# Short score packs of two sequences in one bank, and an earlier send of the second sequence's probabilities, in a latent-attention kernel

## The chip, the cores and the metric

The kernel runs on one core of a Trainium2 chip, in float32. The metric is the device time of one execution in microseconds (us). Five engines work side by side, each through its own list of instructions in order: TensorE (PE in the profile; PEld is its weight load), VectorE (DVE), ScalarE (ACT), GpSimd (POOL) and SyncE (SP, which here only issues transfers). They wait for each other by semaphores. Matrix products go into PSUM banks, from which DVE and ACT read.

## The reference

The input x is 16 sequences of 256 tokens with 256 features. Two layers run one after the other, and each adds (mixer of the normalised x) × silu(feed-forward net of the normalised x) to x. The first layer's mixer is a linear recurrence, and its net a GELU network. The second layer, in which the change lies, has this mixer:

```python
q = (x @ Wq).reshape(B, S, N_HEADS, QK_DIM)             # 16 heads, 128 + 64
q = concatenate([q_nope, apply_rope(q_rope)])
c_kv, k_rope = split(x @ Wkv_a)                         # latent 64, rope 64
k_nope, v = split((rms_norm(c_kv) @ Wkv_b).reshape(...))
scores = einsum('bqhd,bkhd->bhqk', q, k) * scale        # causal mask, softmax
out = einsum('bhqk,bkhd->bqhd', attn, v).reshape(B, S, N_HEADS * V_DIM)
return out @ Wo
```

and, as its net, a linear map with low-rank expert corrections chosen by a router.

## The kernel before

**Tiling.** The 4096 tokens are cut into 8 chunks (`NCH`) of 512 tokens, two sequences each. The kernel multiplies the key and value projections into the query and output weights, so that keys and values are the 64 latent numbers, and a key has 128 rows (64 latent, 64 rope). The 16 heads go in 4 groups of 4. One **unit** is one group of one sequence: 64 units, i = 8 × chunk + r, where even r is the first sequence of the chunk and odd r the second. The main loop has one turn per unit, here called a **slot**, r0 to r7. Later slots of a chunk also carry the router, the keys and the normalisation of the next chunk, and the output product of the chunk before (`fast_begin`, `fast_end`).

**Scores of a unit.** The queries of four heads × 32 positions stand on 128 partitions; there are 8 such query blocks. Block a sees 32·(a + 1) keys, as the mask is causal. The blocks go in three packs, each into one PSUM tile named sc (pool of 3 banks):

```python
PACK = (((7, 0), (6, 256)), ((5, 0), (4, 192), (3, 384)), ((2, 0), (1, 96), (0, 192)))
```

Pack 2, the short one, has blocks of 96, 64 and 32 keys. `score_pack` issues the products of a pack on PE, then on DVE one mask addition and a maximum per block (nm<-sc), then on ACT an exp per block, which writes the probabilities (pr) and their sum (sr). In even slots after i = 4 the short pack is issued as two 64-column tiles per product (128*64 in the profile), elsewhere at full width (128*128). `normalise` inverts sr on DVE and multiplies pr by it on POOL, block by block. pr has two buffers, one for each parity of the unit.

**From probabilities to values.** In the slot after its scores, a unit's pr is turned by three DVE stream transposes (`turn`, with z = 1, 2 from packs 0 and 1, and z = 0 from the short pack), into `turned`. `send` writes it to DRAM in four transfers (far<-turned), and `fetch` brings it back in another layout (pT<-far), two transfers per sequence and group. `values_of` then multiplies both sequences' pT with the values (av), in the even slot that lies two after the group's own. The last two units do the same with PE transposes (`turn_here`).

**Queries.** The products of a group's queries (pq) are made one to three slots ahead, four of them in an even and the odd slot before it: two are multiplied with the rotation on DVE (`query_mul`), added on POOL (`query_rot`, qrot), and brought to their partitions by eight transfers (`query_move`, qg<-qrot); the other two are scaled into qg by ACT (`query_lat`).

**Order.** The helper `InOrder` keeps each engine's instructions in the order in which the program names them, so the loop body is the schedule. All recorded operations carry the helper's line, L53, so groups are told apart by tile names. SP issues sends, fetches and moves from one queue; there are eight semaphores for them in rotation, so a transfer is issued only after the one eight before it has landed. m1, the pool of all other products, has 5 banks.

In the order of one slot: query_move of the group two slots on (even) and fetches; pack 0; normalise of the unit before (pack 2); parts of the gate, the next chunk's layer norm (`norm_end`, in r2 of chunks 1 to 6) and keys; turns 1 and 2 of the unit before; a query product; pack 1; turn 0 and send; in even slots values_of and another fetch; pack 2; normalise (packs 0 and 1); the rest.

Of the kernel before, what the change touches and what calls it, by code (L numbers as in the profile page):

```python
# [11 lines left out]
F32 = mybir.dt.float32  # L12
# [6 lines left out]
P = 128  # L19
B, S, D = 16, 256, 256  # L20
NTOK = B * S
CH = 512
# [19 lines left out]
def tile_two_layers(ctx: ExitStack, tc: tile.TileContext, d: dict, out: bass.AP):  # L42
# [54 lines left out]
    pe = InOrder(nc.tensor)  # L97
# [132 lines left out]
    chunks = [Chunk() for _ in range(NCH)]  # L230
# [150 lines left out]
    NQ = S // 32  # L381
# [4 lines left out]
    groups = [Group() for _ in range(NCH * NG)]  # L386
# [43 lines left out]
    def query_move(n):  # L430
        q = groups[n]
        for r in range(2):
            for h in range(G):
                sp.dma_start(
                    q.qg[64 + 32 * r : 96 + 32 * r, :, h, :],
                    q.rot[32 * h : 32 * h + 32, r, :].rearrange("p (a q) -> p a q", q=32),
                )


    with ExitStack() as l0:  # L440
# [151 lines left out]
        u = tiny("u")  # L592
        f = tiny("f")
# [24 lines left out]
        for k in range(8):  # L618
            n = 1 << k
# [612 lines left out]
        o = out1  # L1232
# [126 lines left out]
    class Unit:  # L1359


        def __init__(self, i):
            self.i = i
            self.ch, r = divmod(i, 2 * NG)
            self.g, self.b = divmod(r, 2)
            self.n = f"{self.ch}_{self.g}_{self.b}"
            self.pr = prs[i % NPR]

    def score_pack(u, pi):
        k, b, pack = chunks[u.ch], u.b, PACK[pi]  # L1370
        if pi == 0:
            u.nm = sm1.tile([P, NQ], F32, tag="nm", name=f"nm_{u.n}", bufs=3)
            u.sr = sm1.tile([P, NQ], F32, tag="sr", name=f"sr_{u.n}", bufs=3)
        qg = groups[u.i // 2].qg
        sc = ps_sc.tile([P, CH], F32, tag="sc", name=f"sc_{u.n}_{pi}")
        halves = 2 if pi == 2 and u.b == 0 and u.i > 4 else 1
        m = P // halves
        for a, o in pack:
            w = qg[:, b * NQ + a, :, :].rearrange("p h q -> p (h q)")
            for y in range(halves):  # L1380
                pe.matmul(
                    sc[m * y : m * y + m, o : o + 32 * (a + 1)], w[:, m * y : m * y + m],
                    k.kT[:, b * S : b * S + 32 * (a + 1)], start=True, stop=True,
                )
        ends = [o + 32 * (a + 1) for a, o in pack]
        step = ends[1] - ends[0]
        n = len(pack)
        assert ends == [ends[0] + step * z for z in range(n)]
        if ends[0] - 32 + step * n <= CH:
            diag = sc[:, ends[0] - 32 : ends[0] - 32 + step * n].rearrange("p (n s) -> p n s", n=n)[:, :, 0:32]  # L1390
        else:
            diag = sc[:, ends[0] - step : ends[-1]].rearrange("p (n s) -> p n s", n=n)[:, :, step - 32 : step]
        ve.tensor_tensor(diag, diag, bc(kmask, n), ALU.add)
        for a, o in pack:
            ve.tensor_reduce(
                u.nm[:, a : a + 1], sc[:, o : o + 32 * (a + 1)], AX.X, ALU.max, negate=True
            )
        for a, o in pack:
            w = 32 * (a + 1)
            ac.activation(  # L1400
                u.pr[:, OFF[a] : OFF[a] + w], sc[:, o : o + w], AF.Exp,
                bias=u.nm[:, a : a + 1], accum_out=u.sr[:, a : a + 1],
            )

    def normalise(u, packs):
        blocks = [a for pi in packs for a, _ in PACK[pi]]
        lo, hi = min(blocks), max(blocks) + 1
        ve.reciprocal(u.sr[:, lo:hi], u.sr[:, lo:hi])
        for a in blocks:
            v = u.pr[:, OFF[a] : OFF[a] + 32 * (a + 1)]  # L1410
            gp.tensor_scalar(v, v, u.sr[:, a : a + 1], 1.0, ALU.mult, ALU.mult)
# [6 lines left out]
    def turn(u, z):  # L1418
        if z == 1:
            u.turned = pp.tile([P, 4, 3, P], F32, tag="turned", name=f"turned_{u.n}", bufs=2)  # L1420
        a0, k0 = THIRDS[z]
        o, w = OFF[a0], WID[a0]
        ve.transpose(
            u.turned[:, :, z, :].rearrange("p k (a q) -> p a k q", q=32),
            u.pr[:, o : o + 4 * w].rearrange("p (a k s) -> p a k s", a=4, s=32)[
                :, :, k0 : k0 + 4, :
            ],
        )
# [15 lines left out]
    def fetch(n, y, b):  # L1444

        q = groups[n]
        if y == b == 0:
            q.pT = {}
        if b == 0:
            q.pT[y] = pp.tile([P, G, 3 * P], F32, tag="pT", name=f"pT_{n}_{y}", bufs=3)  # L1450
        sp.dma_start(
            q.pT[y][64 * b : 64 * b + 64].rearrange("p h q -> p (h q)"),
            q.far[b].rearrange("(y k) s h z q -> y (k s) (h z q)", y=2)[y],
        )

    def turn_here(u, z):

        if z == 1:
            new_pT(u)
        a0, k0 = THIRDS[z]  # L1460
        pt = m1(f"pt_{u.n}_{z}", [P, CH])
        for y in range(4):
            o = OFF[a0] + y * WID[a0] + 32 * k0
            pe.transpose(pt[:, y * P : (y + 1) * P], u.pr[:, o : o + P], ident)
        for y, e in ((0, ac.copy), (2, ve.tensor_copy)):
            e(
                u.pT[:, :, z, 32 * y : 32 * y + 64].rearrange("p h (a q) -> p a h q", q=32),
                pt[:, y * P : (y + 2) * P].rearrange("p (a h q) -> p a h q", a=2, h=G),
            )
# [183 lines left out]
    for i in range(LAST):  # L1653
        ch, r = divmod(i, PER)
        odd = i % 2 == 1
        u, w = units[i], units[i - 1] if i else None
        here = w is not None and w.i >= LAST - 2
        n = (i + 3) // 2 if odd else (i + 2) // 2
        n = n if n < len(groups) else None
        more = ch + 1 < NCH  # L1660
        last = ch - 1 if ch == NCH - 1 and r in FINISH else None
        fast = ch - 1 if 0 < ch < NCH - 1 else None

        if not odd and n is not None:
            query_move(n)
        if odd and i > 2:
            fetch((i - 3) // 2, 0, 1)
            fetch((i - 3) // 2, 1, 1)
        elif i and not odd:
            fetch((i - 2) // 2, 0, 0)  # L1670
        score_pack(u, 0)
        if w:
            normalise(w, (2,))
        if fast is not None and r > 3:
            fast_begin(fast, r)
        if ch > 1 and r == 0:
            fast_begin(ch - 2, 0)
        out_weights(i)
        if r == 1:
            gate_end(ch, 0)  # L1680
        if r == 2:
            gate_end(ch, 1)
            if more and ch:
                norm_end(ch + 1)
        if r == 5 and more:
            kv_end(ch + 1)
        if i == LAST - 1:

            finish_mm(last, 3, 0, NPAIR)
            finish_out(last, 3)  # L1690
            last = None
        if w:
            for z in (1, 2):
                turn_here(w, z) if here else turn(w, z)

        if r == 0:
            mid_chunk(ch)
        if r == 7 and more:
            key_chunk(ch + 1)
        if n is not None:  # L1700
            query_mm(n, 0 if odd else 3)
            if not odd:
                query_lat(n, 3)
        if i == 5:
            values_of(0)
        score_pack(u, 1)

        if odd and n is not None:
            query_mm(n, 1)
            query_mul(n, 0)  # L1710
        if w:
            if here:
                turn_here(w, 0)
            else:
                turn(w, 0)
                send(w)
        if not odd:
            if i > 4:
                values_of((i - 4) // 2)
            if i:  # L1720
                fetch((i - 2) // 2, 1, 0)
        score_pack(u, 2)
        normalise(u, (0, 1))

        if odd and n is not None:
            query_mm(n, 2)
            query_mul(n, 1)
            query_rot(n)
            query_lat(n, 2)
        if r < 2:  # L1730
            gate_begin(ch, r)
        if r == 0 and more and ch:
            norm_begin(ch + 1)
        if r == 2 and more:
            transpose_chunk(ch + 1)
        if r == 4 and more:
            kv_begin(ch + 1)
        if r == 6 and more:
            router_chunk(ch + 1)
        if last is not None:  # L1740
            j = FINISH.index(r)
            finish_mm(last, j, 0, NPAIR)
            finish_out(last, j)
        if fast is not None and r in FINISH:
            fast_end(fast, r)
# [1 line left out]

    ch = NCH - 1
    u0, u1 = units[LAST - 2], units[LAST - 1]
    normalise(u1, (2,))  # L1750

    finish_mm(ch, 0, 0, 4)
    finish_mm(ch, 1, 0, 4)
# [86 lines left out]
```

## Time and profile before

| | |
|---|---|
| median of 3 runs | 903.97 us (903.92 to 904.76) |
| profiled execution | 903.67 us, its span 901.9 us |
| mean granted TensorE clock | 0.994 |
| attention part, first to last slot | 266.49 us to the end |
| one chunk, r0 to r7 (412.71 to 491.50) | 78.79 us |
| slots r0 to r7 of that chunk | 9.41, 10.04, 7.65, 11.03, 11.73, 11.03, 8.23, 9.67 us |

A slot is counted here from PE's first product of its pack 0 to that of the next. The other rows are single instructions or groups on the profile's clock, which starts with the span. A row such as "427.19 0.75 PE … x6" gives the start, the time until the last modelled end, and the number of records; since products overlap in the array, the time that a group holds PE is read from its start to the start of what follows.

### The profile page before, as it was taken

How to read it: one execution, taken by the hardware profiler on the slowest of the kernel's cores; microseconds unless marked ns; L12 is line 12 of the kernel's file. 1: busy time of each engine (PE TensorE's matmuls, PEld its weight loads, DVE VectorE, ACT ScalarE, POOL GpSimd, SP SyncE). 2: the span in 40 equal slices, each digit the busy share in tenths (PEclk: the TensorE clock that was granted, in tenths of full speed). 3: DMA queues.
4: the chain of work that ended last, by engine and by line, in shares of the span. 5: the costliest groups of instructions: out<-in, count | busy, mean ns of one | idle time of the engine just before them, and what ended most of it. 6: DMA issues, size and time to landing. Idle time of an engine off the chain costs nothing.

```text
span 901.9 us, 17976 instructions
## 1 busy us (share of the span) xinstructions
PE 889.3 (99%) x5688; PEld 666.8 (74%) x5688; DVE 667.4 (74%) x2017; ACT 476.0 (53%) x1562; POOL 571.2 (63%) x885
## 2 busy tenths in 40 slices
PE   9999999999999989999999999999999999999988
PEld 8777999987757657776776777677677767766766
DVE  6886678764687869678868867886886788687642
ACT  3234665644436646655655565565556556556441
POOL 2229687787355537787586677758667775876531
PEclk9999999999999999999999999999999999999989
DMA  9730000000024888887887887788788768878880
GB/s 276 245 118 1 1 2 1 1 1 1 1 32 79 230 209 198 186 207 161 217 218 169 206 181 201 180 217 214 170 200 211 190 170 209 210 176 194 209 223 29
DMA packets 197406, 134.04 MB, mean 149 GB/s; under 512 B 143104, under 2 KB 187968, under 8 KB 197312
## 3 DMA queue, kind: packets, MB, share of 16 engines
q1 hardware_dynamic: 195184, 128.69, 58.0%
q0 software_dynamic: 1152, 3.67, 1.2%
q8 instruction: 46, 0.75, 0.4%
q10 hardware_dynamic: 976, 0.53, 0.2%
q14 instruction: 48, 0.39, 0.1%
HBM read 63.11 MB, written 52.95 MB: 129 GB/s over the span
## 4 chain that ended last, share of the span: by engine, by line
PE 93%; DVE 3%; DMA 2%; POOL 1%; ACT 1%; SPq 0%; issue 0%; ACTq 0%; POOLq 0%
PE pq L53 23%; PE sc L53 14%; PE po L53 11%; PE av L53 8%; PE f L53 7%; PE r L53 7%; PE pg L53 5%; PE ph L53 5%; PE pf L53 5%; PE pm L53 2%; PE pkv L53 2%; PE tp L53 2%; DMA far<-turned 1%; DMA pT<-far 1%; PE pb L53 1%; PE py L53 1%
## 5 line engine op out<-in xcount | busy, mean ns | idle before, releaser
L53 POOL TENSOR_SCALAR pr<-pr,sr 128x256 f32<-128x256 f32 (+7 forms) x512 | 192.5, 397 | 188.2 <-DVE sr L53 180.3
L53 ACT ACTIVATE pr<-sc,nm 128x256 f32<-128x256 f32 (+7 forms) x512 | 190.2, 382 | 217.1 <-DVE sr L53 139.6
L53 PEld LDWEIGHTS sc<-kT,qg 128*128 128x128 f32 (+1 forms) x1198 | 150.8, 176 | 54.8 <-issue 41.6
L53 PE MATMUL sc<-kT,qg 128*128 128x32 f32 (+6 forms) x1198 | 169.0, 290 | 0.0
L53 DVE TENSOR_REDUCE nm<-sc 128x1 f32<-128x256 f32 (+7 forms) x512 | 127.5, 301 | 6.6
L53 DVE STREAM_TRANSPOSE turned<-pr 128x512 f32<-128x512 f32 x186 | 123.2, 687 | 11.0 <-POOL pr L53 10.9
L53 PE MATMUL pq<-xnT,wlat 128*128 128x512 f32 x256 | 122.7, 602 | 0.0
L53 PE MATMUL pq<-xnT,wrope 128*128 128x512 f32 x256 | 120.2, 593 | 0.0
L53 ACT ACTIVATION_READ_ACCUMULATOR pr<-sc,nm 128x1 f32 x512 | 104.0, 203 | 0.0
L53 PE MATMUL av<-pT,rowv 64*64 64x512 f32 (+2 forms) x992 | 80.5, 445 | 6.0 <-DMA pT<-far 6.0
L53 POOL TENSOR_TENSOR qrot<-qmul,qmul 128x512 f32<-128x512 f32 x64 | 83.6, 1329 | 2.8 <-DVE qmul L53 2.8
L53 DVE TENSOR_TENSOR sc<-sc,kmask 128x96 f32<-128x96 f32 (+1 forms) x192 | 45.2, 236 | 53.8 <-PE sc L53 52.5
L53 DVE TENSOR_TENSOR qmul<-pq,rot_q 128x512 f32<-128x512 f32 x128 | 80.7, 672 | 0.1
L53 ACT ACTIVATE qg<-pq 64x512 f32<-64x512 f32 x128 | 75.5, 590 | 4.3 <-PE pq L53 3.5
L53 PEld LDWEIGHTS av<-pT,rowv 64*64 64x64 f32 x992 | 39.8, 135 | 43.6 <-issue 30.1
L53 PEld LDWEIGHTS pq<-xnT,wrope 128*128 128x128 f32 x256 | 45.7, 191 | 32.4 <-issue 32.1
L53 PEld LDWEIGHTS pq<-xnT,wlat 128*128 128x128 f32 x256 | 45.7, 191 | 31.6 <-issue 31.6
L53 PEld LDWEIGHTS po<-wout,attT 128*128 128x128 f32 x416 | 59.3, 193 | 9.8 <-issue 3.5
L53 PE MATMUL po<-wout,attT 128*128 128x128 f32 (+1 forms) x416 | 65.3, 311 | 0.0
L53 POOL TENSOR_TENSOR attT<-attT,attT 128x512 f32<-128x512 f32 x36 | 45.1, 1273 | 0.0
L53 POOL TENSOR_TENSOR rs<-ve,mhalf 128x4 f32<-128x4 f32 (+1 forms) x17 | 16.8, 987 | 41.1 <-DVE ve L53 33.6
L53 PE MATMUL pf<-p2T,hT 128*128 128x256 f32 x192 | 42.7, 380 | 0.0
(229 smaller groups left out, 1520.0 us busy)
## 6 DMA issues: line engine op xcount, KB each, us to landing
far<-turned SPq DMA_DIRECT2D x248, 192.0 KB, 4.4
pT<-far SPq DMA_DIRECT2D x124, 384.0 KB, 4.9
qg<-qrot SPq DMA_DIRECT2D x256, 64.0 KB, 2.7
x<-in_x_dram SPq DMA_DIRECT2D x7, 512.0 KB, 10.4
out_dram<-x POOLq DMA_DIRECT2D x12, 256.0 KB, 4.0
wqn_wo<-in_wq_nopeT_dram SPq DMA_DIRECT2D x4, 512.0 KB, 5.4
wqn_wo<-in_Wo_dram SPq DMA_DIRECT2D x4, 512.0 KB, 6.8
p2T<-in_proj2T_dram SPq DMA_DIRECT2D x2, 512.0 KB, 8.3
```

The costliest lines, as they stand in the source:

```text
L53: r = getattr(self.engine, name)(*args, **kw)
```

## The change

`score_pack` is cut into `score_mm` (products) and `score_exp` (mask, maxima, exps). Every short pack is now issued in two 64-column tiles. A new function, `score_small(u, v)`, runs in each even slot: it takes one bank for the short pack of the even unit u (from column 0) and of the next odd unit v (from column 256), issues the 12 + 12 tiled products, and then mask, maxima and exps of u, and after them those of v. Odd slots have no short pack.

The order changes with it. An even slot does all three turns of the odd unit before it ahead of pack 1, and sends it; only then come query_move and the fetch that stood at the slot's start. An odd slot normalises the short packs of both units at its start, since both were made in the even slot before. The tail's normalise of the last unit's short pack falls away.

```diff
+    def score_mm(u, pi, sc, base=0):
+        k, b = chunks[u.ch], u.b
+        qg = groups[u.i // 2].qg
+        m = P // 2 if pi == 2 else P
+        for a, o in PACK[pi]:
+            w = qg[:, b * NQ + a, :, :].rearrange("p h q -> p (h q)")
+            for y in range(0, P, m):
+                pe.matmul(
+                    sc[y : y + m, base + o : base + o + 32 * (a + 1)], w[:, y : y + m],
+                    k.kT[:, b * S : b * S + 32 * (a + 1)], start=True, stop=True,
+                )
...
+    def score_pack(u, pi):
+        sc = ps_sc.tile([P, CH], F32, tag="sc", name=f"sc_{u.n}_{pi}")
+        score_mm(u, pi, sc)
+        score_exp(u, pi, sc)
+
+    def score_small(u, v):
+
+        sc = ps_sc.tile([P, CH], F32, tag="sc", name=f"sc_{u.n}_2")
+        for z, y in enumerate((u, v)):
+            score_mm(y, 2, sc, z * S)
+        for z, y in enumerate((u, v)):
+            score_exp(y, 2, sc, z * S)
...
-        if not odd and n is not None:
-            query_move(n)
         if odd and i > 2:
             fetch((i - 3) // 2, 0, 1)
             fetch((i - 3) // 2, 1, 1)
-        elif i and not odd:
-            fetch((i - 2) // 2, 0, 0)
         score_pack(u, 0)
-        if w:
+        if odd:
             normalise(w, (2,))
+            normalise(u, (2,))
...
         if w:
-            for z in (1, 2):
+            for z in (1, 2) if odd else (1, 2, 0):
                 turn_here(w, z) if here else turn(w, z)
+            if not odd:
+                send(w)
+        if not odd and n is not None:
+            query_move(n)
+        if i and not odd:
+            fetch((i - 2) // 2, 0, 0)
...
-        if w:
+        if odd:
             if here:
                 turn_here(w, 0)
             else:
                 turn(w, 0)
                 send(w)
-        if not odd:
+        else:
             if i > 4:
                 values_of((i - 4) // 2)
             if i:
                 fetch((i - 2) // 2, 1, 0)
-        score_pack(u, 2)
+            score_small(u, units[i + 1])
         normalise(u, (0, 1))
...
-    normalise(u1, (2,))
```

More of the change, by code (lines that the diff above doesn't have):

```diff
@@ L1367, in __init__, with score_exp @@
             self.pr = prs[i % NPR]
-    def score_pack(u, pi):
-        k, b, pack = chunks[u.ch], u.b, PACK[pi]
-        if pi == 0:
+            self.nm = None
+    def score_mm(u, pi, sc, base=0):
[9 more added lines that the diff above has]
+                )
+    def score_exp(u, pi, sc, base=0):
+        if u.nm is None:
             u.nm = sm1.tile([P, NQ], F32, tag="nm", name=f"nm_{u.n}", bufs=3)
             u.sr = sm1.tile([P, NQ], F32, tag="sr", name=f"sr_{u.n}", bufs=3)
[L1374 to L1384, printed above, removed]
+        pack = [(a, base + o) for a, o in PACK[pi]]
         ends = [o + 32 * (a + 1) for a, o in pack]
```

## The prediction

> **What bounds the kernel now.** I read the busy times first, then the chain that ended last.
>
> ```profile
> PE 889.3 (99%) x5688; PEld 666.8 (74%) x5688; DVE 667.4 (74%) x2017; ACT 476.0 (53%) x1562; POOL 571.2 (63%) x885
> PE 93%; DVE 3%; DMA 2%; POOL 1%; ACT 1%; SPq 0%; issue 0%; ACTq 0%; POOLq 0%
> PE av L53 <- DMA pT<-far: 6.0, 3, 3.1
> ```
>
> TensorE (PE) is busy in 99% of the span, and the chain is its own order of work. Its waits name one transfer: the values product (av) waiting for turned probabilities (pT). So time is gained by shorter PE work, and lost by whatever reaches PE late. The same engines, cut into the four slots r0 to r3 of chunk 2 (columns: length, then busy time of each engine):
>
> ```profile
> 412.71:422.12 9.41, 9.41 (x76) 6.70 (x75) 7.62 (x26) 7.70 (x30) 8.67 (x15) 1.00 0.66 145
> 422.12:432.16 10.04, 10.04 (x41) 6.81 (x40) 9.70 (x31) 4.39 (x22) 6.80 (x14) 1.00 0.79 207
> 432.16:439.81 7.65, 7.65 (x67) 5.50 (x66) 7.40 (x18) 3.80 (x10) 5.00 (x8) 1.00 1.00 243
> 439.81:450.84 11.03, 11.03 (x63) 8.11 (x62) 8.14 (x26) 8.07 (x34) 5.84 (x14) 1.00 0.75 179
> ```
>
> PE has no gap, but VectorE (DVE) is at 9.70 of 10.04 in r1 and 7.40 of 7.65 in r2: DVE that enters r1 late is still late in r2, and only r3 (8.14 of 11.03) has room. That decides my forecast. PE's timeline (start, length to the last modelled end, count):
>
> ```profile
> 425.47 1.88 PE L53 MATMUL pq<-xnT,wrope 128*128 128x512 f32 x4
> 427.19 0.75 PE L53 MATMUL sc<-kT,qg 128*128 128x96 f32 x6
> 427.77 1.96 PE L53 MATMUL pq<-xnT,wlat 128*128 128x512 f32 x4
> 429.57 1.03 PE L53 MATMUL pg<-wbase,xnT 128*128 128x256 f32 x4
> ...
> 435.60 2.83 PE L53 MATMUL av<-pT,rowv 64*64 64x512 f32 x32
> 438.36 0.59 PE L53 MATMUL sc<-kT,qg 128*64 128x96 f32 x12
> 438.88 1.09 PE L53 MATMUL tp<-ident,xn 128*128 128x128 f32 x8
> ```
>
> From start to start, a short pack 128 columns wide takes 427.77 − 427.19 = 0.58 us, and the query group behind it 1.80 where the group ahead takes 1.72. The pack in two 64-column tiles takes 438.88 − 438.36 = 0.52. DVE and SP in r2:
>
> ```profile
> 434.97 2.36 DVE L53 TENSOR_SCALAR xn<-x,mv,rs 128x256 f32<-128x256 f32 x4
> 437.25 1.29 DVE L53 STREAM_TRANSPOSE turned<-pr 128x512 f32<-128x512 f32 x2
> 438.47 0.23 DVE L53 TENSOR_TENSOR sc<-sc,kmask 128x96 f32<-128x96 f32 x1
> 438.73 0.79 DVE L53 TENSOR_REDUCE nm<-sc 128x1 f32<-128x192 f32 x3
> 439.44 0.70 DVE L53 STREAM_TRANSPOSE turned<-pr 128x512 f32<-128x512 f32 x1
> ```
> ```profile
> 371.19 2.58 SPq L53 DMA_DIRECT2D far<-turned  x4
> 373.88 6.67 SPq L53 DMA_DIRECT2D qg<-qrot  x8
> ```
>
> SP's stretch, taken from the group at 371, is what the change creates in every even slot: four sends and then the eight query moves without a pause. The last move lands 1.64 after its issue, at 382.19, so 11.0 us from the first send. Such stretches take 10.2 (432.50 to 442.73) to 13.25 us (450.14 to 463.39).
>
> **The change, part by part**, against the profiled execution (903.67 us, span 901.9; the median is 0.3 higher).
>
> 1. *Odd slots lose their short pack*: 32 × (0.58 + 0.08) = −21.1 us of PE.
>
> 2. *Even slots get a second tiled pack.* Both run in one tile mode. Inside the pack of 438.36 the six pairs step by 0.133, 0.083, 0.055, 0.059, 0.031 and then 0.16 until the next product starts. Without the last drain that is 0.36; with it 0.52. I take 0.38, since the entry and the drain are paid once: 32 × 0.38 = +12.2. Units 0, 2 and 4 become tiled too: 3 × −0.15 = −0.4. PE together −9.4 (−5 if the full 0.52 is paid).
>
> The pairs of 96, 64 and 32 columns step by less and less. [...]
>
> 3. *Sends of the odd units come ahead of the moves.* Before, they are issued in the next slot's middle, behind fetches, and SP waits 81.9 us in 65 waits for far. Where data now comes early, old stalls go: av of slot 6 (315.77 to 323.54, 7.8 us, where 2.31 is usual) −5.5; av of slot 62 (859.95 to 867.39, 7.4) −5.1; av in r2 (2.40 to 2.83) −0.3 × 6; slot 8 −0.4. Together −12.8, bounded by 0 if another transfer takes the same place.
>
> 4. *Moves and fetches come behind three turns and four sends*; the moves carry the queries of the slot two later. At the start, slots 2 and 3 are short: turns end at about 288.5, then 2.6 of sends, 5.9 of moves and 1.65 of landing give 298.7 for slot 4's first product, which PE reaches at 295.8: +2.9. At the end, slot 60's turns end at 846.3; sends, moves and four fetches (0.45 to 0.65 each) take until 857, the last lands 4.9 later (median of its row), 862 against 860: +1.85. In r4, r6 and r0 there is margin: in r4 and r6 turns end at 3.3 + 0.65 = 4.0 after the start, so moves land at 15 of some 20 us.
>
> 5. *r2 is the tight one.* Its two slots are the shortest pair (667.99 to 686.21 = 18.22; less 0.28 of part 1 and 2 and 0.09 of av, 17.85), and norm_end stands ahead of its turns. If DVE enters it as before, the turns end at 6.38 + 0.65 = 7.03 after its start, and the moves land at 18.03: 0.18 late.
>
> 6. *DVE enters it late.* In the built order the mask of the second half waits for ACT's last exp of the first, since both lie in one bank. What is queued behind that on DVE: the second half's reduces, a reciprocal, then whatever the slot holds. I follow it on the clock of before from r6 of chunk 2 (473.60) to r2 of chunk 3. In r6 it costs about 1 us (the first half's exps end at 481.85, behind two attT copies of 1.08), ahead of the router's serial chain of 481.10 to 487.38, which fills r7. In r7 POOL does a second short normalise (+0.9) ahead of fast_out's two 1.27 us products, so r0's turns wait for POOL until 496.6 instead of 495.5; with all three now ahead of pack 1's mask they end 7.2 after r0's start. In r0, ACT (7.70 of 9.41 busy) then does pack 1's exps to 500.65, attT to 501.7 and the first half's exps to 502.6, and DVE idles from 500.2. Its gate and norm_begin work moves from 503.5 to 506.0 at the mask that begins r1. r1 gives back 0.73 (its short mask and reduces went) less 0.17, so r2 is entered about 2.2 late, and the turns end near 9.25 after its start.
>
> Then the moves land 9.25 + 11.0 = 20.25 after r2's start, and r4's first product, due at 17.85, waits 2.4. The fetches follow: the moves' issue ends at 17.9, four fetches take 2.2, the last lands 4.4 later (3.8 to 5.4), at 24.45; av is due 3.44 after the first product, at 23.7: +0.75. In r0 a query product also waits for the bank that a late rotation multiply holds, +0.5 (0.4 to 0.65 in this chain). Together 3.65 in each of chunks 1 to 6, where norm_end runs: +21.9.
>
> Within even slots the extra mask and reduces (0.73), and the moved normalises on POOL (63% busy), I cost at nothing beyond this: r3 to r6 have DVE at 5.7 to 8.1 of 8.2 to 11.7 us, which hides them; without that room each 0.73 not hidden would pass on to the next slot's pack.
>
> Sum: −9.4 − 12.8 + 2.9 + 1.85 + 21.9 = +4.45, so 908.1, and 908.4 as a median: 908.
>
> **The rivals.**
>
> *DVE's lateness dies before r2 (faster).* For it: DVE idles 1.8 us in r0 and its idle time moves rather than adds; PE stalls give it time. Against: r1 and r2 hold 0.6 us of room. The sum then has 0.18 + 0.75 in each of six chunks: −9.4 − 12.8 + 4.75 + 5.6 = −11.85, so 892. Between the two the time is linear in the stall: the change breaks even at (9.4 + 12.8 − 4.75) / 6 = 2.9 us per chunk, against 3.65 forecast.
>
> *Sends and moves at their quickest.* With 10.2 us instead of 11.0 the chunk's price is 2.85, and the whole −0.35: 903.6, no change. For it: slot 18's row; against: it began with SP idle, and most are slower.
>
> *They are slow (slower still).* At 13.25, as in the stretch from 450.14 with fetches in flight, r4 waits 2.25 more in each chunk: 908.4 + 13.5, so 922. For it: the DMA share is 1.00 in r2. Against: r2's share holds transfers that will now lie elsewhere.
>
> *The change does not do what it says*: the tiled pairs do not overlap across the two sequences, and the full 0.52 is paid. That is +4.5 on any case, inside the ranges.
>
> [...]
>
> **How the numbers follow.** Forecast (908; own range 904 to 916) 0.44; DVE's lateness dies (892, 886 to 899) 0.31; quickest transfers (903.6, 901 to 906) 0.12; slow ones (922, 914 to 930) 0.13. A measurement of this kernel tells 0.2%, 1.8 us. Faster: 0.31 and 0.04 of the third; within: 0.06 of the third and 0.01; slower: the rest, 0.58. The range 889 to 918 leaves out some 0.08 above and 0.10 below.
>
> **What would show it.** Right: sc rows of 128x32 to 128x96 at 128*128 gone; 24 tiled matmuls in about 0.9 us in each even slot; PE busy some 9 us less; a gap ahead of r4's first sc matmul released by the DMA of qg, 2 to 3 us, in six chunks; DVE idle ahead of the second short mask, released by ACT, about 2 us in r0; no long av in slots 6 and 62. Wrong: no gap at r4 (then 892), gaps at other slots too, or av stalls that remain at the start and the end (up to +10).

## The result and the profile after

The changed kernel takes 936.2 us (median of 6 runs, 927.98 to 937.64) where the kernel before took 904.45 beside it: a ratio of 1.0335, 95% interval 1.0297 to 1.0372. The forecast was slower, 908; the direction held, and the loss was eight times the size. The profiled execution took 937.64 us, its span 935.9.

The page's busy times and the chain that ended last, of the changed kernel:

```profile
PE 905.7 (97%) x5898; PEld 664.2 (71%) x5898; DVE 666.7 (71%) x2017; ACT 474.7 (51%) x1562; POOL 570.8 (61%) x885
PE 55%; DVE 22%; DMA 9%; SPq 4%; ACT 4%; POOL 3%; issue 2%; DVEq 0%; ACTq 0%; POOLq 0%
```

PE's share of the chain fell from 93% to 55%: the end is now set by a loop through turns, sends, moves and fetches. PE is even busy for longer (905.7 against 889.3), although it has less work; part of that is a slower clock (mean granted 0.985 against 0.994; below). PE's waits (total, times, longest):

```profile
PE av L53 <- DMA pT<-far: 14.0, 15, 3.3
PE av L53 <- ACT pr L53: 4.1, 3, 1.5
PE sc L53 <- DMA qg<-qrot: 2.4, 1, 2.4
PE pq L53 <- DVE qmul L53: 1.6, 6, 0.3
```

The product that waits is av, fifteen times instead of three. The first product of r4, which the forecast had waiting for the moves in six chunks, waits only once, at slot 4 (r4 of chunk 0). The rows understate it: in r2 of chunk 3 av holds PE for 4.07 us (528.04 to 532.11) where 2.31 is usual, and the rows list 0.34 of that as idle. The lengths of the slots show the whole (after minus before, profiled executions; "else" is the mean of chunks 1 to 6 without r0 of chunk 1):

| slot | r0 | r1 | r2 | r3 | r4 | r5 | r6 | r7 |
|---|---|---|---|---|---|---|---|---|
| chunk 0 | +0.45 | −0.67 | +0.44 | +1.89 | +2.21 | −0.67 | +0.83 | +0.08 |
| else | +0.90 | −0.67 | +1.97 | −0.63 | +4.31 | −0.67 | +0.40 | −0.67 |
| chunk 7 | +0.90 | −0.67 | +2.41 | −0.67 | +0.17 | −0.67 | +1.11 | −2.05 |

An undisturbed odd slot is 0.67 us shorter, an undisturbed even one 0.40 longer. Beyond that, r0 loses 0.50, r2 1.57 and r4 3.91 in a chunk. PE and SP in chunk 3, from the end of r2's turns to r4 (r2 begins at 524.61):

```profile
544.31 0.97 PE L53 MATMUL sc<-kT,qg 128*128 128x256 f32 x4
...
547.75 1.08 PE L53 MATMUL av<-pT,rowv 64*64 64x512 f32 x4
550.87 3.90 PE L53 MATMUL av<-pT,rowv 64*64 64x512 f32 x28 [2.04 <-DMA pT<-far]
554.70 1.71 PE L53 MATMUL sc<-kT,qg 128*64 128x96 f32 x24
556.33 3.02 PE L53 MATMUL pkv<-wkva,xnT 128*128 128x128 f32 x16
```
```profile
533.43 2.22 SPq L53 DMA_DIRECT2D far<-turned  x4
535.81 5.66 SPq L53 DMA_DIRECT2D qg<-qrot  x8
541.51 3.27 SPq L53 DMA_DIRECT2D pT<-far  x4
```

The third turn ends 8.80 us after r2's start (533.41), the sends go out at 533.43, the moves until 541.47, and four fetches stand behind them. The last move lands at 543.86, before r4 needs it at 544.31. The four fetches land at 546.42, 548.39, 550.74 and 552.05, so av, begun at 547.75, ends at 554.70: 6.95 us instead of 2.31. And what follows is slow as well. The same slot in three stretches (length, busy times of PE, PEld, DVE, ACT and POOL, then the granted clock, the DMA share and GB/s):

```profile
544.31:550.87 6.56, 4.52 (x20) 2.54 (x19) 5.01 (x14) 4.64 (x15) 6.23 (x9) 1.00 1.01 217
550.87:556.33 5.46, 5.46 (x52) 3.68 (x52) 0.00 (x0) 1.07 (x2) 3.16 (x3) 0.56 1.07 327
556.33:562.76 6.43, 6.43 (x50) 6.43 (x49) 2.98 (x15) 2.27 (x13) 2.73 (x6) 0.84 0.81 163
```

After the wait the granted clock is 0.50, from 551.56 to 558.39: the two short packs take 1.63 us instead of 0.92 (470.56 to 471.48 in chunk 2), and pkv 2.86 instead of 1.89.

### The profile page after: what moved, and what is told of

Same layout as the page of the kernel before. It is cut to its first block, busy times and chain, and to the rows that moved or that the text cites. A ratio compares the mean times of both kernels' runs of the same rounds, so it can differ in the third digit from the quotient of the medians.

```text
span 935.9 us, 18355 instructions
## 1 busy us (share of the span) xinstructions
PE 905.7 (97%) x5898; PEld 664.2 (71%) x5898; DVE 666.7 (71%) x2017; ACT 474.7 (51%) x1562; POOL 570.8 (61%) x885
## 4 chain that ended last, share of the span: by engine, by line
PE 55%; DVE 22%; DMA 9%; SPq 4%; ACT 4%; POOL 3%; issue 2%; DVEq 0%; ACTq 0%; POOLq 0%
PE pq L53 9%; DMA pT<-far 7%; PE f L53 7%; PE r L53 7%; PE po L53 6%; PE sc L53 6%; PE av L53 5%; DVE turned L53 5%; DVE nm L53 4%; PE ph L53 4%; PE pf L53 4%; SPq L53 4%; DVE qmul L53 3%; ACT pr L53 3%; DMA qg<-qrot 2%; PE pkv L53 2%
## 5 line engine op out<-in xcount | busy, mean ns | idle before, releaser
L53 PEld LDWEIGHTS sc<-kT,qg 128*64 128x64 f32 (+1 forms) x1408 | 137.3, 164 | 45.1 <-issue 31.1
L53 PE MATMUL sc<-kT,qg 128*64 128x96 f32 (+7 forms) x1408 | 158.8, 279 | 3.0 <-DMA qg<-qrot 2.4
L53 DVE TENSOR_TENSOR sc<-sc,kmask 128x64 f32<-128x64 f32 (+1 forms) x192 | 46.1, 240 | 124.9 <-PE sc L53 68.8
L53 DVE STREAM_TRANSPOSE turned<-pr 128x512 f32<-128x512 f32 x186 | 120.3, 684 | 11.7 <-POOL pr L53 7.3
L53 PE MATMUL av<-pT,rowv 64*64 64x512 f32 (+2 forms) x992 | 100.1, 468 | 18.7 <-DMA pT<-far 14.0
L53 PEld LDWEIGHTS av<-pT,rowv 64*64 64x64 f32 x992 | 43.8, 139 | 71.7 <-issue 29.4
L53 PEld LDWEIGHTS pq<-xnT,wlat 128*128 128x128 f32 x256 | 48.6, 192 | 49.5 <-issue 46.2
L53 ACT COPY attT<-av 128x512 f32<-128x512 f32 x63 | 33.9, 596 | 27.0 <-PE av L53 27.0
```

What stands on the lines that cost most here:

```text
L53: r = getattr(self.engine, name)(*args, **kw)
```

## The experiments

Ratios are against runs of the kernel before on the same chip. Diffs are against the changed kernel unless another is named.

**Which of the two: SP's order or VectorE's wait?** Theory A says that moves and fetches are late since they stand behind the turns; theory B that VectorE's wait for the shared bank makes everything late.

```diff
+        if not odd and n is not None:
+            query_move(n)
+        if i and not odd:
+            fetch((i - 2) // 2, 0, 0)
         if odd and i > 2:
...
-        if not odd and n is not None:
-            query_move(n)
-        if i and not odd:
-            fetch((i - 2) // 2, 0, 0)
```

> The changed kernel with one thing undone: the eight query moves and the first fetch stand at the even slot's start again, ahead of the three turns and the four sends. Theory A, the order on SP's queue (the fetches that stand behind turns, sends and moves land late, and the values product waits for them): the long av groups of r2 and r4 go, PE idles under 3 us in the chunks together, and the time is 890 to 900. Theory B, VectorE's wait on the shared bank (turns, and with them sends, are late whatever SP does): the sends still leave 7 to 9 us after the start of r0 and r2, av still waits, and the time stays above 915.

908.45 us, ratio 1.0050 (1.0032 to 1.0069). Of the 32 us, some 26 are gone by this edit alone (2.85% of 904): r4 is back to +0.39, and av waits 5.0 us in 4 waits instead of 14.0 in 15. r2 still loses: +1.28 to +2.13, +1.60 in the mean. A is right on the large part; its 890 to 900 was not reached, since r0 keeps its loss and r2 most of it, and slots 6 and 62 do not improve (+1.29, −0.30).

```diff
-        sc = ps_sc.tile([P, CH], F32, tag="sc", name=f"sc_{u.n}_2")
+        sc = [ps_sc.tile([P, CH], F32, tag="sc", name=f"sc_{y.n}_2") for y in (u, v)]
         for z, y in enumerate((u, v)):
-            score_mm(y, 2, sc, z * S)
+            score_mm(y, 2, sc[z])
         for z, y in enumerate((u, v)):
-            score_exp(y, 2, sc, z * S)
+            score_exp(y, 2, sc[z])
```

> The changed kernel with the short packs of the two sequences in two banks, so that the mask of the second need not wait for ScalarE's exps of the first; the order on SP is that of the changed kernel. Theory A: r2's three turns end a little earlier (7 to 8 us after its start instead of 9.0), but moves and fetches are still behind them, so the time falls only to 918 to 930. Theory B: the turns of r0 and r2 end 2 us earlier, av no longer waits, and the time is 895 to 908.

918.61 us, ratio 1.0150 (1.0118 to 1.0182): A's range. VectorE's waits in the changed kernel and, in r0 of its chunk 3, the one that the forecast described:

```profile
DVE sc L53 <- ACT pr L53: 55.9, 32, 2.5
DVE turned L53 <- POOL pr L53: 7.3, 9, 1.0
```
```profile
513.49 0.49 DVE L53 TENSOR_REDUCE nm<-sc 128x1 f32<-128x96 f32 x3
516.51 0.27 DVE L53 TENSOR_TENSOR sc<-sc,kmask 128x96 f32<-128x96 f32 x1 [2.54 <-ACT pr L53]
```

With two banks the first row is absent, r2's third turn ends at 6.96 instead of 8.80 after its start, and r4 loses 0.8 to 1.8 instead of 3.91. So the wait is real and worth some 17 us here, but only in this order of transfers: once the moves come first, what it costs is no longer clear of the intervals (see the table below). r2 as a whole is no shorter (+2.15 in the mean against the kernel before).

```diff
-            for z in (1, 2) if odd else (1, 2, 0):
+            for z in (1, 2):
                 turn_here(w, z) if here else turn(w, z)
-            if not odd:
-                send(w)
...
-        if odd:
+        if w:
             if here:
                 turn_here(w, 0)
             else:
                 turn(w, 0)
                 send(w)
...
```

(with the moves and the fetch first, as in the first run)

> The shared, tiled short packs of the changed kernel in the transfer order of the kernel before: moves and fetch first, third turn and send after pack 1. Theory A: PE's 9.4 us are gained and the stalls at slots 6 and 62 are those of the kernel before: 893 to 898. Theory B: the wait on the shared bank makes turns and sends late in r0 and r2, so 905 to 925.

910.39 us, ratio 1.0073 (1.0047 to 1.0099): within B's range, outside A's. Sending the odd unit early or late makes hardly a difference (908.45 against 910.39), so the 12.8 us that the forecast put down to early sends are not there. Something else than the transfer order costs as well.

The kernel before, with the changed order alone:

```diff
-        if not odd and n is not None:
-            query_move(n)
...
-        elif i and not odd:
-            fetch((i - 2) // 2, 0, 0)
...
-            for z in (1, 2):
+            for z in (1, 2) if odd else (1, 2, 0):
                 turn_here(w, z) if here else turn(w, z)
+            if not odd:
+                send(w)
+        if not odd and n is not None:
+            query_move(n)
+        if i and not odd:
+            fetch((i - 2) // 2, 0, 0)
...
-        if w:
+        if odd:
             if here:
                 turn_here(w, 0)
```

> The kernel before with only the transfer order of the changed kernel (three turns and the send ahead of the moves and the fetch in even slots), its short packs where they were, so that no bank is shared and VectorE has no new wait. Theory A: the fetches are late all the same, av waits in r2 and r4, and the time is 918 to 940. Theory B: 900 to 908.

929.16 us, ratio 1.0278 (1.0236 to 1.0320): theory A's range, without any shared bank. Here it is r2 that loses most, 2.1 to 3.1 us, and r4 0.5 to 1.3.

**What costs the rest?** First the price of tiling by itself, on the kernel before:

```diff
-        halves = 2 if pi == 2 and u.b == 0 and u.i > 4 else 1
+        halves = 2 if pi == 2 else 1
```

> The kernel before with nothing but every short pack in two 64-column tiles, where it stood. The rows of before price a full-width pack at 0.66 us and a lone tiled one at 0.52, so 35 x 0.14 = 4.9 us less, all of it on TensorE: 898 to 900. If tiling a small dimension brings nothing (the rival to that price), 903 to 905.

905.75 us, ratio 1.0017 (0.9991 to 1.0043). Every odd slot is 0.05 us longer. A tiled pack alone, between full-width products, costs as much here as a full-width one (0.71 us against 0.66); the 0.27 us of a pair come from two packs that stand together.

Then both causes undone (the first two diffs together):

> The changed kernel with both causes undone: moves and first fetch at the slot's start, and the two short packs in two banks. If the order on SP and the wait on the shared bank are the two causes (theory C, after the first four runs), r0 and r2 lose their stalls, slots change by -0.67 (odd) and +0.40 (even) against the kernel before, and the time is 893 to 898. Theory D, that GpSimd's two short normalises at the odd slot's start delay qrot and with it the moves as well: r2 keeps a stall of about 1 us, and the time is 899 to 905.

908.09 us, ratio 1.0039 (1.0017 to 1.0061). The second bank brings nothing more that is clear of the intervals once the moves are first. Theory C fails, and D's 899 to 905 is missed as well. Theory D puts the rest down to the normalises; the next kernel is the one before with only the odd unit's short pack moved:

```diff
-        score_pack(u, 2)
+        if not odd:
+            score_small(u, units[i + 1])
         normalise(u, (0, 1))
```

(`score_small` with two banks; all short packs tiled; `normalise(w, (2,))` where it was before)

> The kernel before with only the odd unit's short pack made in the even slot, tiled, in a bank of its own: turns, sends, moves, fetches and normalises as before. Theory C: 893 to 898, the same as with the normalises at the odd slot's start. Theory D: 893 to 896 here, and at least 4 us more there.

901.8 us, ratio 0.9975 (0.9949 to 1.0002), outside the ranges of C and D, and with one bank:

> As the last, but the two short packs share one bank. Against the last it prices the wait on the shared bank alone, with the order of before. Theory C: VectorE's wait in r0 and r2 makes turns and sends late, 3 to 8 us in all, so 898 to 904. If the bank matters only behind late moves (rival), within 2 us of the last.

903.07 us, ratio 0.9992 (0.9967 to 1.0017), 1.3 us from the two-bank run, which the rival had (within 2) and theory C's range does not exclude. D is right about the difference, though not about the times: 6.3 us between the two-bank kernels that differ in turns and normalises, and 7.3 between the one-bank kernels that differ in the normalises alone (910.39 and 903.07; in the profiled executions, 5.1 apart, r0 and r2 hold 3.5 of it). GpSimd in r7 and r0 of chunk 3, first with both short normalises at the odd slot's start (r0 begins at 493.89), then with one (490.44):

```profile
492.16 1.76 POOL L53 TENSOR_SCALAR pr<-pr,sr 128x96 f32<-128x96 f32 x6 [4.07 <-DVE sr L53]
493.88 1.28 POOL L53 TENSOR_TENSOR c<-c,g 128x512 f32<-128x512 f32 x1
...
499.63 2.50 POOL L53 TENSOR_TENSOR qrot<-qmul,qmul 128x512 f32<-128x512 f32 x2
```
```profile
488.72 0.90 POOL L53 TENSOR_SCALAR pr<-pr,sr 128x96 f32<-128x96 f32 x3 [4.07 <-DVE sr L53]
489.58 1.27 POOL L53 TENSOR_TENSOR c<-c,g 128x512 f32<-128x512 f32 x1
...
495.33 2.50 POOL L53 TENSOR_TENSOR qrot<-qmul,qmul 128x512 f32<-128x512 f32 x2
```

qrot starts 5.74 us after r0's start instead of 4.89, and the moves wait for it. The 0.86 us for the second normalise, which the forecast charged to the turns alone, are paid by the queries too.

The steps in a row, each with one thing more, as ratios to the kernel before (the third lies within the intervals of the second):

| packs shared, two banks | + turns early, normalises at the odd slot's start | + one bank | + moves and fetch behind the turns |
|---|---|---|---|
| 0.9975 | 1.0039 | 1.0050 | 1.0335 |

**Can the normalises go where GpSimd idles?** Edits on the two-bank kernel at 901.8, and then one of them on the kernel before:

```diff
-        if w:
+        if odd and r != 7:
             normalise(w, (2,))
         if fast is not None and r > 3:
             fast_begin(fast, r)
+        if odd:
+            normalise(u, (2,))
...
+        if r == 6:
+            normalise(u, (2,))
         if r == 6 and more:
             router_chunk(ch + 1)
```

> The two-bank packs in the order of before, and three short normalises placed where GpSimd idles: the one of r6 ahead of the router's chain, so that GpSimd need not wait 5 us in r7 for VectorE's reciprocal behind that chain, and each odd unit's in its own slot. Theory E (after eight runs: the stretch from r7 to r3 is held by VectorE, GpSimd and SP, so a shorter TensorE gives nothing there until one of them is relieved): VectorE's idle 1.4 us ahead of r0's third turn goes, r2 loses 0.5 to 1 us in each of six chunks, and the time is 895 to 899. Rival: r2 is held by SP's transfers alone, so nothing changes: 900 to 903.

910.32 us, ratio 1.0065 (1.0041 to 1.0088): slower than either expected.

```diff
-        if w:
+        if w and r != 7:
             normalise(w, (2,))
...
+        if r == 6:
+            normalise(u, (2,))
         if r == 6 and more:
             router_chunk(ch + 1)
```

> The kernel before with only r6's short normalise ahead of the router's chain. TensorE has no gap there in the kernel before, so theory E expects no more than the small av stalls of r2 back: 901 to 904. If GpSimd's wait in r7 costs TensorE time already (rival), 897 to 900.

915.26 us, ratio 1.0126 (1.0087 to 1.0166), slower than either expected too, from one reciprocal and its normalise that moved. VectorE and GpSimd in r6 and r7 of chunk 2:

```profile
483.18 0.18 DVE L53 RECIPROCAL sr<-sr 128x3 f32<-128x3 f32 x1 [1.05 <-ACT pr L53]
...
485.31 1.32 DVE L53 SCALAR_TENSOR_TENSOR l<-oh,lg 128x32 f32<-128x32 f32 x1
...
486.89 1.08 DVE L53 TENSOR_TENSOR eq<-l,m 128x32 f32<-128x32 f32 x1
```
```profile
485.32 1.26 POOL L53 TENSOR_TENSOR c<-c,g 128x512 f32<-128x512 f32 x1
486.66 1.26 POOL L53 TENSOR_TENSOR x<-x,c 128x512 f32<-128x512 f32 x1
```

The reciprocal waits 1.05 us for ACT with the router's chain behind it, but that costs nothing: the chain's second product lg stands 8.47 us after r6's start, 8.43 in the kernel before. GpSimd's two-operand products, now early, run beside that chain: two operations that take 0.19 us in the kernel before take 1.32 and 1.08. VectorE is 2 us later, and PE loses 0.5 in r7 and 0.82 in r0 of most chunks. GpSimd's idle time there was not free.

**Where does the shorter PE time count?** The two-bank packs in the order of before, shared in two groups of each chunk only (elsewhere tiled as in the kernel before):

```diff
+    def shared(i):
+        return i >= PER and i % PER // 2 in SHARE
...
-        score_pack(u, 2)
+        if not shared(i):
+            score_pack(u, 2)
+        elif not odd:
+            score_small(u, units[i + 1])
```

With `SHARE = (1, 2)`, the groups of r2 and r4:

> The two-bank packs in the order of before, but shared only in the groups of r2 and r4 of chunks 1 to 7; the groups of r0 and r6 keep each sequence's pack in its own slot. Theory E (TensorE's saving counts only where the other engines have room, r3 to r6): -0.27 in each of 14 groups, less up to 0.1 where r3's first pack waits for a bank, so -2.5 to -3.8 us: a ratio of 0.9958 to 0.9972. Rival (the saving is lost wherever it is made, to the transfers' own pace): 0.999 to 1.001.

907.25 us, ratio 1.0014 (0.9995 to 1.0032). With `SHARE = (0, 3)`, those of r0 and r6:

> The same, but shared only in the groups of r0 and r6 of chunks 1 to 7, the same count of packs. Theory E: VectorE has no room from r7 to r2, so the packs' extra VectorE work ahead of the router's chain and of norm_begin costs what TensorE gains: a ratio of 0.999 to 1.003. Rival (groups are alike): that of the other run within 0.001.

902.91 us, ratio 0.9975 (0.9956 to 0.9994). Theory E was the wrong way round. r0 and r1, and r6 and r7, each pair is 0.27 shorter; it is the group of r2 that loses: r2 grows by 1.1 to 1.7 us, of which 0.40 is the pack and r3 gives back 0.57. One cause stands at r3's start in the former kernel:

```profile
522.30 1.08 PE L53 MATMUL sc<-kT,qg 128*128 128x256 f32 x4 [0.60 <-ACT pr L53]
```

The two packs hold two of the three score banks while r2's late VectorE work keeps ACT from emptying them. This wait is 0.60 of the 1.05 us that r2 loses there beyond the pack; the rest is not shown. So r2's group is left out, `SHARE = (0, 2, 3)`:

> The two-bank packs in the order of before, shared in the groups of r0, r4 and r6 of chunks 1 to 7; r2's group, where the last two runs showed a wait for a score bank of 0.4 to 1.2 us at r3's start, keeps its packs. Theory H (only that bank wait and the transfers ahead of r2's av take the saving away): -0.27 in each of 21 groups, less 0.3 to 0.6 in r2, so -1.5 to -4 us and a ratio of 0.995 to 0.998. Rival (a shorter TensorE gives nothing anywhere): 0.999 to 1.001.

902.71 us against 905.73, ratio 0.9969 (0.9951 to 0.9987). That is within theory H's range and faster than both kernels, the one before by 0.3%; the intervals do not set it apart from `SHARE = (0, 3)`. In its profile r0/r1, r4/r5 and r6/r7 are each 0.27 shorter in chunks 2 to 6, and r2 is −0.08 to +1.68.

**Which late transfer is waited for?** One fetch of the changed kernel, moved alone:

```diff
+        if i and not odd:
+            fetch((i - 2) // 2, 0, 0)
         if odd and i > 2:
...
-        if i and not odd:
-            fetch((i - 2) // 2, 0, 0)
```

> The changed kernel with a single transfer moved: the first fetch stands at the even slot's start, ahead of turns, sends and moves, which all stay late. Theory F (the failed term is the landing of four fetches in a row, 1.8 us apart, which the values product of r2, r4 and slot 62 waits for): three in a row land 1.8 us earlier, av of r2 and r4 waits less by 1 to 2 us each, most of the clock's drops go, and the time is 915 to 926. Rival G (the late moves are what costs): nothing changes, 930 to 938.

939.97 us, ratio 1.0377 (1.0358 to 1.0395): neither F nor G, at a mean clock of 0.991 to 0.995. PE's waits and SP in r2 of chunk 3 (527.04):

```profile
PE sc L53 <- DMA qg<-qrot: 12.2, 6, 3.0
PE av L53 <- DMA pT<-far: 6.9, 14, 1.3
```
```profile
526.84 3.14 SPq L53 DMA_DIRECT2D far<-turned  x4
535.12 0.45 SPq L53 DMA_DIRECT2D pT<-far  x1
535.67 2.74 SPq L53 DMA_DIRECT2D far<-turned  x4
538.51 6.23 SPq L53 DMA_DIRECT2D qg<-qrot  x8
544.85 1.85 SPq L53 DMA_DIRECT2D pT<-far  x3
```

av waits half as long, and r4 is 0.35 to 4.3 us shorter than in the changed kernel, as F has it: the last of three fetches lands 6.6 us after its issue, not 7.3. But the fetch reads what the sends before it write, and SP holds it until they have landed (534.98), with the next sends and moves behind it, though the third turn ended at 534.11. Now the first products wait for the moves. Of the orders tried with late moves, each leaves a wait for some late transfer; the earlier start of the moves and the fetch, as in the first run, took r4's away.

## Why the prediction was wrong

The step that failed is how the forecast followed transfers through SP's queue: it let early sends remove 12.8 us of stalls (part 3), which did not come, and it followed late moves and fetches only to r4, with too quick a landing (parts 4 and 5), where the values products of r2 and r4 waited for the last of four fetches.

- **PE's work** was priced well: −0.67 per odd slot (forecast −0.66), +0.40 per even slot (+0.38). Units 0, 2 and 4 gained nothing (about +0.05, forecast −0.15), as tiling in place brought nothing (ratio 1.0017). The step took the 0.52 of a lone tiled pack from even slots, where it follows av, which is tiled too; between full-width products it costs 0.71 (0.66 + 0.05). Why a lone pack loses 0.05 where a pair gains 0.27 is not shown. About 0.9 us of the miss.
- **VectorE's lateness** (part 6) came as described: idle 2.54 us in r0 (2.4), r0's turns 7.4 after its start (7.2), r2's 8.8 to 9.0 (9.25), a query product late in r0 with 0.50 per chunk (0.5). The rival that it dies before r2 fell.
- **Part 3 failed.** "Where data now comes early, old stalls go", −5.5 and −5.1: slots 6 and 62 became 0.83 and 1.11 longer. The bound that this part named, another transfer in the same place, fits: SP issues or waits without a pause from 291 to 333 us in the kernel before, and in the run with the order alone slot 6 is 3.2 us shorter but slots 3 and 4 together 4.3 longer. With the 1.85 of part 4 and 0.40 of PE work each already counted, these two slots make 9.9 us of the miss. That size is loose: in four profiled executions whose program is the same in chunk 0 (the kernel before and the three `SHARE` runs), slot 6 lasts 13.7 to 17.7 us. But in no run is it more than 3.3 us shorter than in the kernel before, nor slot 62 more than 2.2.
- **The landing of the fetches** (parts 4 and 5) was mis-sized. I took 4.4 to 4.9 us after issue, the middle of rows in which two fetches follow each other. Four in a row (issued from 541.51) landed 1.3 to 2.4 us apart, the last 7.3 after issue. In r4 of chunk 3 the last landed 27.4 us after r2's start, where 24.45 was forecast. The start of part 4 was right: slot 4 began at 298.72 (298.7).
- **r0's own chain was not followed to r2.** I did not hold the fetches behind its moves against r2's av: 1.57 us lost in r2 where −0.3 was forecast, 11.2 in six chunks. In chunk 3 these four land 1.1, 2.9, 4.7 and 6.5 us after r2's start, and av begins at 3.4. That lateness hid the wait of r4's first product which I forecast at 2.4. What it takes to free r2 is shown only in part: beyond the 0.40 of the pack it still loses 1.2 with the moves first, 1.7 with two banks as well, and 0.9 in the order of before with one normalise. In chunk 3 of the first run the last two fetches go out at 514.39, just after r1's sends have landed (514.25).
- **The clock** had no term. r4 lost 3.91 instead of 3.15 per chunk, 4.6 in all, and in chunk 3 some 1.7 of its 6.3 is the halved clock (0.71 at the short packs, 0.97 at pkv). An order can be as slow without it: the order-alone run took 929 us and the one-fetch run 940 with profiles at a clock of 0.994, that of the kernel before.

9.9 + 11.2 + 4.6 + 0.9 = 26.6; the profiled execution was 29.5 above its forecast (937.6 against 908.1), and the rest lies in the other slots of chunks 0 and 7. A cost that I put at the turns alone, the second short normalise, also delays qrot and the moves, which the runs with the order undone show as 6 to 7 us together with the early turns, or alone.

## What to carry to other kernels

When a step is put ahead of others on a queue, follow the last transfer behind it, not the first: time it to its landing with the spacing of the whole row, and hold it against the product that reads it one and two stages on. On a queue that is busy throughout, as here, an early place for one step is a late one for another. And a saving on the busiest engine should be priced together with what its new place holds up on every other engine: here the move of 0.27 us a pair was clear of the interval only with two banks, one normalise where it had been, and r2's group left out.

## What the runs showed of the hardware

- **After some of PE's waits the granted clock halved.** In the changed kernel gaps in PE's records of 2.39 us (before 298.72), 1.60 (322.14), 2.36 (384.18), 2.04 (550.87), 1.36 (718.29) and 3.25 (899.38) were followed by a granted clock of 0.50, while gaps of 1.54 (802.11) and, in the order-alone run, 1.95 (444.33) were not. The low clock lasted 3.41 us (298.97 to 302.39, and after three other gaps) or 6.83 (551.56 to 558.39, and after 322.14). The six low stretches begin at 298.97, 322.87, 384.31, 551.56, 718.81 and 899.72, which are 7, 18, 49, 49 and 53 times 3.413 us apart; that this would let like gaps end differently is my guess, which no run tested. The spread of the changed kernel's runs goes with the clock: 927.98 us at a mean clock of 0.996, 937.64 at 0.985.
- **Fetches issued in a row landed later and later.** Issued 0.6 us apart, they landed 3.6, 4.9, 6.6 and 7.3 us after their issue had ended (slot 27 of the changed kernel, with the DMA share at 1.01 in the stretch from 544.31; 3.9 and 4.9, medians of 31 rows, for two in a row in the kernel before).
- **Two VectorE operations lengthened beside GpSimd's two-operand products.** In the run with one early normalise on the kernel before, l<-oh,lg took 1.32 us (from 485.31) and eq<-l,m 1.08 (from 486.89), each 0.19 in the kernel before. Beside them ran c<-c,g (485.32) and x<-x,c (486.66), of 1.26 us each, and both VectorE operations ended 0.05 us after the product beside them.
